# Graph-network layer on one core: convolution groups of 116 columns from whole batches, and of 116 to 136 columns from parts of one row of blocks

## The chip, the core and the metric

The kernel runs on one core of a Trainium2 chip. The core has five engines with queues of their own: TensorE (PE; PEld is its weight load) multiplies matrices into PSUM, VectorE (DVE) and ScalarE (ACT) work elementwise, GpSimd (POOL) and SyncE (SP) mostly issue DMAs here. An engine takes its instructions in the order in which they were written, and waits on semaphores for other engines and for DMAs. The metric is the device time of one execution in microseconds (us).

## The reference

x is [32, 512, 256], 32 batches of 512 nodes with 256 features; adj is a 0/1 mask [32, 512, 512]; everything is float32.

```python
h = maximum(layernorm(x), 0)
# convolution branch, per batch
c = relu(bn1(conv1d(h.T, conv1_w)))              # 1 tap, 256 -> 256 channels
c = bn2(conv1d(c, conv2_w, pad=8))               # 17 taps, 256 -> 256 channels
x_conv = relu(c + h.T).T                         # residual
# graph branch
s = h @ w_se.T + b_se                            # 3 numbers per node
A = exp(-squared_distance(s, s)) * adj
x_nmp = A @ relu(h @ w_msg.T + b_msg)
# gates (GRU cell)
gi = concat([x_conv, x_nmp]) @ w_ih.T + b_ih
gh = h @ w_hh.T + b_hh
r = sigmoid(gi_r + gh_r); z = sigmoid(gi_z + gh_z)
n = tanh(gi_n + r * gh_n)
out = x + (1 - z) * n + z * h
```

## The kernel before

**Layout.** Channels lie on the 128 partitions, in ND = 2 halves; the 512 positions of a batch lie along the free dimension. Two memory spaces matter: SBUF, and PSUM with 8 banks of 512 float32 a partition. The PSUM pools are cps (2 banks, tile ps_c), bps (1 bank, ps_b), acc (2 banks, ps_acc) and gps (3 banks, ps_g).

**The convolution of 17 taps** is done with a two-level fast scheme. A batch is cut into U = 29 blocks of Q = 18 outputs. From a group's input h1 (18 phases; one column per block, channel half and batch), VectorE forms 25 operands x2 (`fives` twice: five combinations of combinations); each operand is multiplied with its own combination of weights w, and 25 products are added into 9 sums y (`summed`, `both`). The weights of the 25 products are made once, during group 0, and kept in DRAM (WD); later groups load them again, 768 KB a product. A group is G = 4 whole batches, so 4 x 29 = 116 columns and NG = 8 groups; each row of blocks has one spare column (V = 30).

In group 0 a product is 16 matmul calls of two terms. From group 1 on it is three small products: psb (tile ps_b) of the operand's middle with the sum of both weights, which ScalarE copies out as mid, and two products of the differences xd (`ends`, VectorE), which fill the two halves of one bank ps_c. `both` adds mid to both halves and brings them to SBUF (VectorE). That makes 12 matmul calls; each float32 matmul call is two instructions on TensorE, so 24 instructions a product. Both cps banks alternate from product to product. `sums.send(done)` hands product n to `both` after ps_b of product n+1.

When a group is done, `evacuate` (ScalarE, batch norm folded in) writes each batch's 512 outputs per channel half from y into a tile xconv, of which there are four; it waits with batch b until batch b - 4 has passed its gates. `convolution` waits before the sixth product of a group until all evacuations of the last one are done.

**The other streams** are Python generators: `rows` (conv1 of a batch, which fills h1), `begins` (norm and transpose of a batch, hT, also stored in DRAM as hd), `graphs` (messages, kernel matrix, masks; its result goes to DRAM as nd) and `gates` (per batch 36 products in the order ps_r, ps_h, ps_z, ps_n for each channel half o; 144 instructions on TensorE). The gates need hTb (h again, from hd), xnb (from nd) and xconv. At the head of a batch, `residual` adds hTb to xconv on VectorE, then ScalarE applies relu; the first gate products run beside it, the products with xconv wait for it.

**Order.** A planner written out in the kernel orders the work while it is built. It keeps a model time `now` and, per engine, the time `free`; it always takes the next piece of the stream whose clock is least among those that are ready (`streams` holds each stream's rate and offset). `fill` slips VectorE background work in (norms, operands, weights, `sum_some`) as long as VectorE's model time is less than 1.5 us ahead, and `LATER` holds actions with due times. This order is what each engine's queue gets; real waits come from semaphores.

Two helpers carry nearly all instructions, so the profile names their lines: L127 for every matmul, L118 for every VectorE and ScalarE operation, L132 for transposes on TensorE. L740 are the kernel matrix's small matmuls, L929 the stores of the output, L768 the stores of nd.

Of the kernel before, what the change touches and what calls it, by code (L numbers as in the profile page):

```python
# [8 lines left out]
F32 = mybir.dt.float32  # L9
# [24 lines left out]
V = U + 1  # L34
Q = 18
TURNED = 8
# [8 lines left out]
def kernel(  # L45
# [27 lines left out]

    nc = tc.nc
# [3 lines left out]
    NG = B // G  # L78
    NR = ND * G
    NU = G * U  # L80
    NH = ND * NU
    NZ = 2 * NH
    RV = NR * V
# [5 lines left out]
    cps = ctx.enter_context(tc.tile_pool(name="cps", bufs=2, space=PSUM))  # L89
# [67 lines left out]
    XD_ = {b: dram.tile([N, D], F32, name=f"xd{b}") for b in range(TURNED, B)}  # L157
    ND_ = {(b, d): dram.tile([P, N], F32, name=f"nd{b}_{d}") for b in range(B) for d in range(ND)}
# [25 lines left out]
    def load_gates(b):  # L184
        if b >= B or b in HB:
            return
        HB[b] = late.tile([P, ND, N], F32, name="hTb", bufs=2)
        nc.sync.dma_start(HB[b], HD[b])

# [47 lines left out]
    h1 = const.tile([P, Q, NR, V], F32)  # L237
    for q, v in ((slice(0, LEAD), slice(0, 1)), (slice(Q - 1, Q), slice(V - 2, V - 1)), (slice(0, Q), slice(V - 1, V))):
        nc.gpsimd.memset(h1[:, q, :, v], 0.0)
# [88 lines left out]
    def conv1(b, o):  # L328
        hT = HT[b] if b < G else HR[b]
        ps = bank()  # L330
        matmul_sum(ps, [(w1[:, i, o * P : (o + 1) * P], hT[:, i, :]) for i in range(ND)])

        r, h = o * G + b % G, V - 2
        blocks = ps[:, : Q * h].rearrange("p (v q) -> p q v", q=Q)
        for dst, src in (
            (h1[:, LEAD:, r, :h], blocks[:, :LEAD, :]),
            (h1[:, :LEAD, r, 1 : h + 1], blocks[:, LEAD:, :]),
            (h1[:, LEAD : LEAD + N - Q * h, r, h], ps[:, Q * h :]),
        ):
            act.activation(  # L340
                dst, src, AF.Relu, bias=bn1_sh[:, o : o + 1], scale=bn1_sc[:, o : o + 1],
            )


    def fives(src, n, new):
# [8 lines left out]
        def sub(dst, a, b):  # L354
            some = n if a < 3 else n - 1
            dve.tensor_tensor(dst[:, :some, :], get(a, some), get(b, some), op=ALU.subtract)
            if a > 2:
                at = [src[:, 3 * n - 3 + b, :], flat[:, (b - 3) * RV + 1 : (b - 2) * RV + 1]]
                dve.tensor_tensor(
                    dst[:, some, :], flat[:, (a - 3) * RV + 1 : (a - 2) * RV + 1], at[b > 2],  # L360
                    op=ALU.subtract,
                )
# [7 lines left out]
        for a, b in ((2, 0), (4, 2)):  # L370
            t = new()
            sub(t, a, b)
            yield None
            if b == 0:
                less2(t, t, d1)
            else:
                less2(t, d1, t)
            yield t
# [11 lines left out]
    def operands():  # L390

        for x1 in fives(
            h1.rearrange("p q r v -> p q (r v)"), 6,
            lambda: cv.tile([P, 6, RV], F32, name="x1", bufs=3),
        ):
            yield None
            if x1 is not None:
                yield from fives(x1, 2, lambda: cv.tile([P, 2, RV], F32, name="x2", bufs=6))

    def ends(x2):  # L400

        xd = cv.tile([P, 2, RV], F32, name="xd", bufs=2)
        d0 = x2[:, 0, :]
        d02 = bass.AP(d0.tensor, d0.offset, [d0.ap[0], (1, 2), (1, RV)])
        dve.tensor_tensor(
            xd, d02, x2[:, 1:2, :].to_broadcast([P, 2, RV]), op=ALU.subtract
        )
        return xd
# [83 lines left out]
    SUMS = []  # L492

    def sum_all():
        while SUMS:
            SUMS.pop(0)()
        settle()

    def summed(g):

        y = None

# [13 lines left out]
        def both(dst, got):  # L518

            ps, mid = got  # L520
            if mid is None:
# [3 lines left out]
                dst.rearrange("p (h n) -> p h n", h=2), ps.rearrange("p (h n) -> p h n", h=2),  # L525
                mid[:, None, :].to_broadcast([P, 2, NH]), op=ALU.add,
            )

        for j1 in ORDER:
            got = yield  # L530
            n3 = cv.tile([P, NZ], F32, name="n", bufs=3)
# [3 lines left out]
            z = cv.tile([P, 3, NZ], F32, name="z")  # L535
# [7 lines left out]
            n2 = cv.tile([P, NZ], F32, name="n", bufs=3)  # L543
            both(n2, got)
            got = yield
            n1 = cv.tile([P, NZ], F32, name="n1")
# [3 lines left out]
            add(zends, zends, n1[:, None, :].to_broadcast([P, 2, NZ]))  # L550
            more(z[:, 1, :], n3, 2.0, n2)
            if j1 == 3:
                y = cv.tile([P, 3, 3, NZ], F32, name="y")
# [9 lines left out]
            (dve.free + 0.3, y, b, o) for b in range(g * G, (g + 1) * G) for o in range(ND)  # L563
# [4 lines left out]

    def evacuate():

        t, y, b, o = EVAC[0]
        if now < t or b >= G and b - G not in gated or act.free > now + 0.3:
            return False
        EVAC.pop(0)
        if o == 0:
            XC[b] = late.tile([P, ND, Q * U], F32, name="xconv", bufs=4)
        c = o * NU + b % G * U
        act.activation(
            XC[b][:, o, :].rearrange("p (u h k) -> p k h u", h=2, k=9),
            y.rearrange("p e f (h n) -> p (e f) h n", h=2)[:, :, :, c : c + U],  # L580
            AF.Identity, bias=bn2_sh[:, o : o + 1], scale=bn2_sc[:, o : o + 1],
        )
        if o == ND - 1:
            evacuated[b] = act.free + LAG
# [3 lines left out]
    XC, evacuated, gated = {}, {}, set()  # L588
# [4 lines left out]
    def all_operands():  # L593
        for _ in range(NG):
            yield from operands()
# [27 lines left out]
    def convolution():  # L623
# [3 lines left out]
        def sides(t, first=0):  # L627
            return t.rearrange("p (r v) -> p r v", v=V)[:, :, first : first + U]

        def product(ps, *terms):  # L630

            for o in range(ND):
                matmul_sum(
                    ps[:, o * NU : (o + 1) * NU].rearrange("p (b u) -> p b u", u=U),
                    [
                        (w[:, k, i, o * P : (o + 1) * P], rows[:, i * G : (i + 1) * G, :])
                        for k, rows in terms
# [3 lines left out]

        for g in range(NG):
            sums = summed(g)
            next(sums)
            done = None
            for n in range(25):
                at_product = m = 25 * g + n
                if n == 5:
                    yield lambda: not EVAC
# [7 lines left out]
                for k in (m, m + 1):  # L657
                    if 25 <= k < len(X2) and k not in XD:
                        XD[k] = ends(X2[k])
# [6 lines left out]
                ps = cps.tile([P, N], F32, name="ps_c")[:, :NZ]  # L666
                if g == 0:
                    d0, d1, d2 = sides(x2[:, 0, :]), sides(x2[:, 1, :]), sides(x2[:, 0, :], 1)
                    product(ps[:, :NH], (0, d0), (1, d1))
                    if done is not None:  # L670
                        sums.send(done)
                    yield now
                    product(ps[:, NH:], (0, d1), (1, d2))
                    mid = None
                else:
                    psb = bps.tile([P, N], F32, name="ps_b")[:, :NH]
                    product(psb, (2, sides(x2[:, 1, :])))
                    mid = cv.tile([P, NH], F32, name="mid", bufs=2)
                    act.activation(mid, psb, AF.Copy)
                    if done is not None:  # L680
                        sums.send(done)
                    yield now
                    for k in range(2):
                        product(ps[:, k * NH : (k + 1) * NH], (k, sides(XD[m][:, k, :])))
                    del XD[m]
                WS[m] = X2[m] = None
                done = ps, mid
                at_product = m + 1
                yield now
            sums.send(done)  # L690
# [135 lines left out]
    def rows(b):  # L826
        nonlocal made, made_at
        for o in range(ND):
            conv1(b, o)
            if o == ND - 1 and b % G == G - 1:  # L830
                made, made_at = b // G + 1, act.free + LAG
# [36 lines left out]
    def gates(b):  # L868
# [25 lines left out]

        def residual():
            xconv = XC.pop(b)[:, :, :N]
            dve.tensor_tensor(xconv, xconv, hT, op=ALU.add)
            yield dve.free + 0.3
            act.activation(xconv, xconv, AF.Relu)
            x_in.extend([xconv[:, i, :] for i in range(ND)] + [XN[b, d] for d in range(ND)])  # L900
# [35 lines left out]
        for o in range(ND):  # L936
# [30 lines left out]
            if o == 0:  # L967
                yield lambda: b in evacuated
                yield evacuated[b]
                yield from residual()  # L970
                yield from products(ps_r, o, 0, 0, 1, (0, 2))
                yield act.free + LAG
# [7 lines left out]
            if o == 0:  # L980
                load_gates(b + 1)
            ps_n = acc.tile([P, N], F32, name="ps_acc")
# [16 lines left out]
        gated.add(b)  # L999
# [4 lines left out]
    def sum_some():  # L1004
        if not SUMS:
            return False
        SUMS.pop(0)()
        return True

    def norm_ahead(early=0.45):  # L1010
        for b in list(NORMS)[:2]:
            if (b < G or clock["conv"] >= (b - G) / G - early) and norm_some(b):
# [40 lines left out]
    def all_rows():  # L1053
        nonlocal rows_wait
        for b in range(B):
            if b < G:
                yield from begin(b)
                yield act.free + LAG
            else:
                yield lambda: freed >= b // G - 1 and begun > b  # L1060
# [3 lines left out]
            yield from rows(b)  # L1064
            rows_wait = False

    def all_gates():
# [9 lines left out]
        "begins": (all_begins(), 4.2, -0.15),  # L1077
        "graphs": (all_graphs(), 49.0, 0.0),
        "conv": (convolution(), 66.0, 0.0),
        "gates": (all_gates(), 125.0, 1.25),  # L1080
# [19 lines left out]
    spare = cv.tile([P, 3, 3, NZ], F32, name="y").rearrange("p e f n -> p (e f n)")  # L1100
# [84 lines left out]
```

## Time and profile before

| | |
|---|---|
| median of 4 runs | 2148.93 us (2144.97 to 2149.88) |
| the profiled execution | 2147.35 us, its span 2145.5 us |
| TensorE busy | 2090.0 us (97%), 9200 instructions; weight loads 1293.8 us |
| VectorE busy | 1525.5 us (71%) |
| ScalarE busy | 761.6 us (35%) |
| GpSimd busy | 298.8 us (14%) |
| DMA | 367.12 MB, mean 171 GB/s; the queue that SP issues to carries 282.95 MB |

The page of a profile gives busy times by engine, then 40 slices of the span (each digit is tenths of busy time). The chain of waits follows the work that ended last back to its start. A group of instructions has the form: line, engine, operation, out<-in, shape, count | busy time of the group, mean ns of one | idle time of the engine before them and what ended it. Matmuls overlap in the pipeline, so the mean of one (277 ns for 116 columns) is longer than the time by which the next one follows; how long one holds the engine is read from the chain, or from the group's busy time over its count.

### The profile page before, as it was taken

Reading aid. Unit: us, or ns where it says so; the run is one execution under the profiler, and the core shown is the slowest. Engines: PE = TensorE matmul, PEld = TensorE weight load, DVE = VectorE, ACT = ScalarE, POOL = GpSimd, SP = SyncE. Lnnn points to the kernel's source line nnn. Section 1 sums busy time; section 2 is a strip of 40 time slices with the busy share of each in tenths; the row PEclk is TensorE's granted clock in tenths of the full one; section 3 lists DMA queues with packets and bytes.
Section 4 is the critical chain, followed back from the end, with each engine's and each line's share of the span. In section 5 each row is a group of like instructions: output and inputs, shape, how many; then the busy total and the mean of one; then the engine's idle time right before and its main releaser. Section 6 shows DMA issues by size and latency. Waiting matters only on the chain.

```text
span 2145.5 us, 26566 instructions
## 1 busy us (share of the span) xinstructions
PE 2090.0 (97%) x9200; PEld 1293.8 (60%) x9200; DVE 1525.5 (71%) x2820; ACT 761.6 (35%) x1277; POOL 298.8 (14%) x446
## 2 busy tenths in 40 slices
PE   8988989999999999999999999999999999999998
PEld 4876666566665666556665666656665566665443
DVE  6897778677776877667885777767776677776333
ACT  5635432433233442234324252342522334222311
POOL 2100121111111111101111111110111010011111
PEclk9999999999999999999999999999999999999999
DMA  7446666657676576766766757766675565554232
GB/s 277 178 162 240 190 188 187 206 161 195 160 211 182 157 191 192 203 167 182 199 178 187 210 134 200 198 180 177 177 195 148 152 165 153 143 156 95 59 69 40
DMA packets 539478, 367.12 MB, mean 171 GB/s; under 512 B 455248, under 2 KB 472016, under 8 KB 538704
## 3 DMA queue, kind: packets, MB, share of 16 engines
q1 hardware_dynamic: 511408, 282.95, 48.9%
q0 software_dynamic: 23248, 69.23, 10.3%
q10 hardware_dynamic: 4688, 13.24, 1.6%
q8 instruction: 73, 1.20, 0.2%
q14 instruction: 61, 0.50, 0.1%
HBM read 282.74 MB, written 82.58 MB: 170 GB/s over the span
## 4 chain that ended last, share of the span: by engine, by line
PE 83%; ACT 1%; DVE 1%; issue 0%; DVEq 0%; ACTq 0%
PE ps_acc L127 44%; PE ps_g L127 17%; PE ps_c L127 14%; PE ps_b L127 7%; PE ps_b L740 1%; PE ps_g L132 1%; ACT at L118 0%; DVE xconv L118 0%; ACT xconv L118 0%; ACT L118 0%; DVE r L118 0%; DVE o_sb L118 0%; PE ps_g L740 0%; DVE msg L118 0%; DVE res L118 0%
## 5 line engine op out<-in xcount | busy, mean ns | idle before, releaser
L127 PE MATMUL ps_acc<-xconv,wih 128*128 128x512 f32 (+1 forms) x772 | 362.6, 592 | 5.2 <-ACT xconv L118 5.2
L127 PE MATMUL ps_acc<-xnb,wih 128*128 128x512 f32 (+1 forms) x772 | 362.5, 592 | 0.0
L127 PE MATMUL ps_acc<-hTb,whh 128*128 128x512 f32 x768 | 355.5, 593 | 0.1
L127 PE MATMUL ps_c<-xd,w 128*128 128x116 f32 x2800 | 344.3, 277 | 5.2 <-DVE z L118 5.2
L127 PEld LDWEIGHTS ps_c<-xd,w 128*128 128x128 f32 x2800 | 329.9, 193 | 7.9 <-DVE z L118 5.5
L929 POOL DMA_DIRECT2D out_dram<-res x252 | 164.2, 657 | 908.7 <-DVE res L118 854.5
L118 DVE TENSOR_TENSOR r<-ps_acc,r 128x512 f32<-128x512 f32 (+1 forms) x65 | 44.4, 683 | 337.4 <-PE ps_acc L127 337.4
L127 PEld LDWEIGHTS ps_acc<-xnb,wih 128*128 128x128 f32 x772 | 142.0, 189 | 164.4 <-issue 163.5
L127 PEld LDWEIGHTS ps_acc<-xconv,wih 128*128 128x128 f32 x772 | 141.6, 190 | 158.9 <-issue 147.8
L127 PE MATMUL ps_g<-at,msg 128*128 128x512 f32 x512 | 229.2, 598 | 4.9 <-DVE at L118 4.9
L127 PEld LDWEIGHTS ps_acc<-hTb,whh 128*128 128x128 f32 x768 | 141.6, 190 | 147.7 <-issue 143.3
L127 PEld LDWEIGHTS ps_b<-x,w 128*128 128x128 f32 x1400 | 181.9, 191 | 73.2 <-issue 55.6
L118 ACT ACTIVATE mid<-ps_b 128x232 f32<-128x232 f32 x175 | 63.9, 365 | 377.3 <-PE ps_b L127 344.7
L127 PE MATMUL ps_b<-x,w 128*128 128x116 f32 x1400 | 183.6, 274 | 6.7 <-ACT at L118 6.7
L127 PEld LDWEIGHTS ps_g<-at,msg 128*128 128x128 f32 x512 | 96.9, 192 | 122.1 <-issue 113.5
L118 DVE SCALAR_TENSOR_TENSOR x<-x,x 128x480 f32<-128x480 f32 (+1 forms) x184 | 144.1, 783 | 3.4
L118 DVE TENSOR_TENSOR x<-x 128x240 f32<-128x240 f32 (+1 forms) x320 | 134.3, 461 | 0.6
L127 PE MATMUL ps_g<-wmsg,hTg 128*128 128x259 f32 x496 | 124.5, 383 | 0.0
L127 PE MATMUL ps_g<-hT,w 128*128 128x512 f32 x256 | 119.4, 610 | 1.2 <-ACT at L118 1.2
L118 ACT ACTIVATE z<-ps_acc,brz 128x512 f32<-128x512 f32 x64 | 44.0, 687 | 214.3 <-PE ps_acc L127 214.2
L127 PEld LDWEIGHTS ps_g<-wmsg,hTg 128*128 128x128 f32 x496 | 92.9, 191 | 43.0 <-issue 31.8
L118 DVE TENSOR_TENSOR xd<-x 128x480 f32<-128x480 f32 x175 | 113.1, 648 | 3.3 <-PE ps_c L127 3.3
(109 smaller groups left out, 2475.7 us busy)
## 6 DMA issues: line engine op xcount, KB each, us to landing
w<-wd SPq DMA_DIRECT2D x150, 768.0 KB, 5.6
m_sb<-in_adj_dram SPq DMA_DIRECT2D x384, 64.0 KB, 2.6
hd<-hT POOLq DMA_DIRECT2D x32, 512.0 KB, 6.1
hTb<-hd SPq DMA_DIRECT2D x32, 512.0 KB, 4.9
xnb<-nd SPq DMA_DIRECT2D x64, 256.0 KB, 2.9
res<-in_x_dram SPq DMA_DIRECT2D x256, 64.0 KB, 3.1
out_dram<-res POOLq DMA_DIRECT2D x252, 64.0 KB, 3.2
hTg<-hd SPq DMA_DIRECT2D x31, 512.0 KB, 4.3
```

What stands on the lines that cost most here:

```text
L118: getattr(self.engine, name)(*tiles, **more)
L127: nc.tensor.matmul(ps, lhsT, rhs, **more)
L132: nc.tensor.transpose(ps, a, ident)
L740: nc.tensor.matmul(pss[c], gr.left[k, :], gr.right[k, :], start=True, stop=True, tile_position=(32 * c, 0),)
L929: queue.dma_start(OB[b][:, s.start // 32 : s.stop // 32, o * P + 32 * g : o * P + 32 * g + 32], y[at, s].rearrange("i (k j) -> i k j", j=32),)
```

## The change

The batches are laid side by side as one row of 32 x 29 = 928 blocks, which is cut at 116, 251, 386, 522, 657, 792: seven groups, of 116, 135, 135, 136, 135, 135 and 136 columns. A cut may fall inside a batch; such a batch's conv1 runs twice, each time for the columns that its group needs. Between channel halves there is one spare column, and the zeros at the batches' ends are set for each group (`zeros`, on GpSimd). A product's halves have up to 272 columns each, and both do not fit one bank; ps_c becomes one tile of two banks, and there is one of it (cps has bufs=1). In group 0, where 232 + 232 columns fit a bank, products alternate between its two banks. `hand` gives a product to `both` at once (0.3 us of model time later) or, at the latest, after the next ps_b.

Evacuation goes into small tiles part (three of them), from which a DMA on POOL's queue brings the piece to DRAM (CD, `cd`). `load_conv` brings a batch's xconv back (SP's queue, two tiles), while the batch before is at its gates; `residual` adds and applies relu there, after the ps_z products of the batch before's second half. The tiles for x1 and n are fewer (2 for 3), n1 lies in z. The planner's offsets and rates follow the new group length; the gates' offset goes from 1.25 to 1.6 groups.

```diff
-V = U + 1
+STARTS = (0, 116, 251, 386, 522, 657, 792, 928)
+NG = len(STARTS) - 1
+UG = max(j - i for i, j in zip(STARTS, STARTS[1:]))
+PER = (STARTS[-1] - STARTS[1]) / (NG - 1) / U
...
-    cps = ctx.enter_context(tc.tile_pool(name="cps", bufs=2, space=PSUM))
+    cps = ctx.enter_context(tc.tile_pool(name="cps", bufs=1, space=PSUM))
...
+    CD = {b: dram.tile([P, ND, N], F32, name=f"cd{b}") for b in range(B)}
...
+    def load_conv(b):
+        if b < B and b not in XC and evacuated.get(b, 1e9) <= now:
+            XC[b] = late.tile([P, ND, N], F32, name="xconv", bufs=2)
+            nc.sync.dma_start(XC[b], CD[b])
+            XC_AT[b] = now + 7.0
+
+    def residual(b):
+        if b not in XC or b in RES or now < XC_AT[b]:
+            return
+        dve.tensor_tensor(XC[b], XC[b], HB[b], op=ALU.add)
+        RES[b] = 1e9
+
+        def relu():
+            act.activation(XC[b], XC[b], AF.Relu)
+            RES[b] = act.free + LAG
+
+        later(dve.free + 0.3, relu)
...
+    def zeros(g):
+        at = input_of(g)
+        for b in range(B + 1):
+            v = U * b - STARTS[g]
+            if 0 <= v <= sizes(g)[0]:
+                nc.gpsimd.memset(at[:, : Q if v == sizes(g)[0] else LEAD, :, v : v + 1], 0.0)
+                if v > 0:
+                    nc.gpsimd.memset(at[:, Q - 1 : Q, :, v - 1 : v], 0.0)
...
         for j1 in ORDER:
             got = yield
-            n3 = cv.tile([P, NZ], F32, name="n", bufs=3)
+            sum_all(read)
+            n3 = columns("n", bufs=2)
             both(n3, got)
...
-        t, y, b, o = EVAC[0]
-        if now < t or b >= G and b - G not in gated or act.free > now + 0.3:
+        t, y, g, b, o = EVAC[0]
+        if now < t or act.free > now + 0.3:
             return False
...
+        part = late.tile([P, Q * U], F32, name="part", bufs=3)[:, : Q * (last - first)]
         act.activation(
...
+        n0, n1 = Q * first, min(Q * last, N)
+        later(act.free + 0.4, lambda: nc.gpsimd.dma_start(CD[b][:, o, n0:n1], part[:, : n1 - n0]))
+        if o == ND - 1 and last == U:
+            evacuated[b] = act.free + 4.0
...
+        def hand():
+            nonlocal done
+            if done is not None:
+                got, done = done, None
+                sums.send(got)
...
-                if n == 5:
+                if n == 4:
                     yield lambda: not EVAC
...
-                ps = cps.tile([P, N], F32, name="ps_c")[:, :NZ]
...
+                    psb = bps.tile([P, N], F32, name="ps_b")[:, :nh]
+                    product(psb, (2, x2[:, 1, :], 0))
+                    mid = cv.tile([P, NH], F32, name="mid", bufs=2)[:, :nh]
                     act.activation(mid, psb, AF.Copy)
-                    if done is not None:
-                        sums.send(done)
+                    hand()
                     yield now
+                    ps = cps.tile([P, 2, N], F32, name="ps_c")[:, :, :nh]
                     for k in range(2):
-                        product(ps[:, k * NH : (k + 1) * NH], (k, sides(XD[m][:, k, :])))
+                        product(ps[:, k, :], (k, XD[m][:, k, :], 0))
                     del XD[m]
                 WS[m] = X2[m] = None
                 done = ps, mid
+                if g > 0:
+                    later(now + 0.3, hand)
...
             if o == 0:
-                yield lambda: b in evacuated
-                yield evacuated[b]
-                yield from residual()
+                if b not in XC:
+                    yield lambda: b in evacuated
+                    yield evacuated[b]
+                    load_conv(b)
+                yield XC_AT[b]
+                residual(b)
                 yield from products(ps_r, o, 0, 0, 1, (0, 2))
-                yield act.free + LAG
+                yield lambda: RES[b] < 1e9
+                yield RES[b]
...
             if o == 0:
                 load_gates(b + 1)
+                load_conv(b + 1)
+            else:
+                residual(b + 1)
...
+        for g in range(1, NG):
+            for b in batches(g):
+                yield lambda: freed >= g - 1 and begun > b
+                if b == batches(g)[0]:
+                    zeros(g)
                 rows_wait = True
                 load_row(b)
                 yield now + 8.0
-            yield from rows(b)
-            rows_wait = False
+                yield from rows(g, b)
+                rows_wait = False
...
-        "begins": (all_begins(), 4.2, -0.15),
-        "graphs": (all_graphs(), 49.0, 0.0),
-        "conv": (convolution(), 66.0, 0.0),
-        "gates": (all_gates(), 125.0, 1.25),
+        "begins": (all_begins(), 1.05 * PER, -0.15),
+        "graphs": (all_graphs(), 11.5 * PER, 0.0),
+        "conv": (convolution(), 80.0, 0.0),
+        "gates": (all_gates(), 31.25 * PER, 1.6),
```

## The prediction

> **What bounds the kernel now.** I read the shares by engine first, then the slices and TensorE's waits, then the chain of waits.
>
> ```profile
> PE 2090.0 (97%) x9200; PEld 1293.8 (60%) x9200; DVE 1525.5 (71%) x2820; ACT 761.6 (35%) x1277; POOL 298.8 (14%) x446
> ...
> PE   8988989999999999999999999999999999999998
> ...
> DVE  6897778677776877667885777767776677776333
> ```
>
> TensorE works 97% of the span, nearly evenly. VectorE follows at 71%, with most load early: 83.08 us of the 100 between 300 and 400 us. TensorE's own waits are few:
>
> ```profile
> PE ps_b L127 <- ACT at L118: 6.7, 8, 1.6
> PE ps_acc L127 <- ACT xconv L118: 5.2, 4, 1.4
> PE ps_c L127 <- DVE z L118: 5.2, 2, 3.0
> PE ps_g L127 <- DVE at L118: 4.9, 3, 2.7
> ```
>
> (us, times, longest.) So the kernel becomes faster only through less TensorE work, as long as no new waits appear. How long one instruction holds TensorE is read from the chain of waits in stretches without gaps (start us, us, what):
>
> ```profile
> 606.77 0.88 PE ps_b L127 x8
> 607.65 1.79 PE ps_c L127 x16
> 609.44 5.16 PE ps_acc L127 x12
> ...
> 638.00 0.88 PE ps_g L127 x4
> ```
>
> ```profile
> 664.88 0.55 PE ps_g L132 x5
> ```
>
> Per instruction: 512 columns take 5.16/12 = 430 ns, 259 columns (the messages) 0.88/4 = 220 ns, 128 columns (transposes) 0.55/5 = 110 ns, and the convolution's 116 columns 2.67/24 = 111 ns. From 128 columns up, time goes with columns at 0.839 ns (430/512), and a small rest: 259 x 0.839 = 217, 128 x 0.839 = 107. But 116 columns should take 97 ns, and take as long as 128. There is a floor, and the convolution lies on it. The groups of instructions name a likely floor:
>
> ```profile
> L127 PE MATMUL ps_c<-xd,w 128*128 128x116 f32 x2800 | 344.3, 277 | 5.2 <-DVE z L118 5.2
> L127 PEld LDWEIGHTS ps_c<-xd,w 128*128 128x128 f32 x2800 | 329.9, 193 | 7.9 <-DVE z L118 5.5
> ```
>
> The weight loads fill 329.9 us of the 344.3 us of these matmuls: each 116-column matmul needs a load of 128 weight columns, and this load is as long as it.
>
> **The change, part by part.** The sum is made against the profiled execution, 2147.35 us (span 2145.5), which lies 1.6 us below the median of the four runs.
>
> *Fewer, wider products.* Group 0 stays at 116 columns. Behind it 7 groups of 25 products become 6, at 135 or 136 columns (mean 135.3). Before: 175 products x 24 instructions x 111.3 ns = 467 us. After: 150 x 24 = 3600 instructions. By the slope one takes 135.3 x 0.839 = 113.5 ns, with the rest of 2.5 ns that 128 and 259 columns show 116 ns; 3600 x 116 = 418 us. Gain 49 us. The ends: 113.5 ns gives 58 us; if the 14 ns above the streaming time were a cost of every instruction and no floor, 135.3 columns would take 127.5 ns and the gain would be 8 us. I take 116, since 128 columns are nearest and show no such cost.
>
> *VectorE work* of the convolution has the same columns in fewer instructions. Its operations x take 653 ns for 480 columns and 1651 for 1440, so 154 ns of each are fixed; the changed kernel issues 2660 VectorE instructions where 2820 were: 160 x 154 ns = 25 us less. VectorE is not on the path, so this only makes room.
>
> *One buffer for a product's output instead of two.* A product's two halves now have a bank each, and there is one pair: product n+1 may not write ps_c before VectorE has added mid and read product n out. One such read of 464 columns took 632 ns; 540 take some 715. Behind the waiting matmul stand all others, on an engine that keeps its order. What covers it is the TensorE work between the two. From the new order of TensorE, with the durations above: in 137 of the 150 products 2.6 us or more stand between, mostly 6 to 8. In 10 only the next product's ps_b (8 x 116 ns = 0.93 us) stands between, in 3 more 1 to 2.6 us; all 13 lie in group 1 and the first two thirds of group 2, where VectorE is fullest. The same kernel before has 6 such close pairs, and the two waits for z (2.20 and 2.96 us) are among them although it has two buffers. So a close pair costs at least 5.2/6 = 0.87 us, and at most about 3.0. I take 1.5, as only part of VectorE's queue is ahead of the read: 13 x 1.5 = 19.5, less the 5.2 of before: +14 us (ends +6 and +34). Why not more elsewhere: VectorE's longest wait in sum is the one for ps_acc, 402.4 us, so it is mostly ahead of TensorE.
>
> [...] The order of the instructions says that other streams' matmuls cover the evacuation in 137 cases.
>
> *Residual made ahead.* Its add and relu stood between a batch's last products and the next's. The chain shows what that cost once TensorE had nothing else:
>
> ```profile
> 2039.40 0.69 DVE r L118
> 2040.09 1.14 DVE xconv L118
> ...
> 2041.26 1.07 ACT xconv L118
> ...
> 2042.37 29.46 PE ps_acc L127 x68
> ```
>
> The four waits sum to 5.2 us. They now run a stage earlier, beside the ps_n products (8 x 430 ns = 3.4 us, more than 1.14 + 1.07). Gain 5 us (0 to 6); next in line there is nothing late.
>
> *Outputs through DRAM.* 72 pieces instead of 64 evacuations (1323 ns each on ScalarE, before and after); each then goes out on POOL's queue, and 32 loads of 512 KB come in on SP's. Three piece buffers: ScalarE's fourth must wait until the first has left. Nearest row: 256 KB stores of nd from POOL land 2.9 and 2.5 us after issue; issue itself takes some 0.57 us. So a buffer is busy 1.3 + 3.5 + about 0.5 us, while two more evacuations take 2.6: ScalarE can be held 0 to 2 us each time, and with it mid and the gate sigmoids queued behind. ScalarE is 35% busy and TensorE has two ps_acc banks (1.7 us of products to a bank), so only the excess shows. Ends 0 and 72 x 0.5 = 36; I take +4, as the nearest rows (mid starting promptly behind 1.3 us evacuations without a TensorE wait for it) lie near zero. On SP the new load waits for the store, with the loads of w and masks behind it; it is issued only when the planner thinks the piece is out, and 25 loads of 768 KB disappear: 0 (to +5). POOL gains 72 issues of 0.6 us and 64 tiny memsets at 14% load: 0 to 3, I take 1; behind them in its queue stand out_dram and nd, which nobody waits for soon.
>
> [...]
>
> *Seams.* Four batches are split by a group's end: their conv1 is computed with 18 columns of overlap, 32 instructions x 15 ns: +0.5 us, and 4 more loads of hT. Group 1 needs five batches instead of four before it can start, group 2 six; a load and rows take about 10 us a batch, in place of 40 us now 50 to 60, against about 8 products (some 90 us) between the freeing of h1 and its next need. The start of group 1 (TensorE worked 91.06 of 100 us between 200 and 300) can lose up to 10: I take +3.
>
> Sum: -49 + 14 - 5 + 4 + 1 + 0.5 + 3 = -31.5, so 2147.35 becomes 2116; against the median of the runs that is 2117.
>
> **Rivals.**
> 1. *Nothing new shows*: the close pairs fall together with waits that exist anyway. -58 - 6: 2083 to 2095. For it: VectorE gets lighter. Against: 13 close pairs where it is fullest.
> 2. *ScalarE is held by the pieces*, or the trip through DRAM is late for the gates: another +20: 2132 to 2144. For: pieces follow each other in the new order of ScalarE, with mid between them. Against: other streams stand ready.
> 3. *Slower: the single output buffer.* If reads come late not in 13 but in most products, the convolution pays each time. It decides from (49 + 5 - 8)/150 = 0.31 us a product; at 0.5 us: 2147 - 46 + 75 = 2176. For: the read is queued behind whatever VectorE has, up to two or three operations of 0.7 to 1.7 us. Against: 6 to 8 us between.
> 4. *The floor is none* (8 us gain): 2147 - 8 - 5 + 22 = 2156. Against: the 110 ns of 128 columns.
>
> **Chances and range.** Forecast (2097 to 2132) 0.57, as its terms are rows and counts; rival 1 0.14; rival 2 0.14; rival 3 0.09; rival 4 0.04; 0.02 other. 0.2% (4.3 us) is about what the runs tell from no change. Same gets 0.03, from the upper part of rival 2 and from rival 4; slower 0.11; faster 0.86. Range 2088 to 2150: rivals 3, 4 and a part of 1 stay outside. Likeliest alone: 2097 to 2132.
>
> **What would show it.** ps_b and ps_c of 135 columns at 2.75 to 2.8 us a product; 3600 instructions where 4200 were; waits of ps_c for n and z of 10 to 30 us, between 200 and 560 us; no waits for xconv in the last batches; ScalarE waiting for DMAs before its pieces, with TensorE hardly touched. Waits for ps_c spread over the whole span, or a pitch over 120 ns, would prove me wrong.

## The result and the profile after

The changed kernel takes 2151.54 us (median of 47 runs, 2145.14 to 2163.55), the kernel before 2148.7 (71 runs); the ratio is 1.0015, 95% interval 1.0009 to 1.0021. The forecast of 2117 us is wrong: nothing was gained. The ratio of an experiment below is taken to the kernel before as measured beside it (2150.2 to 2150.4 us). The span of the profiled execution is 2149.8 us.

The page after, the lines that answer to those of before:

```profile
PE 2058.6 (96%) x8632; PEld 1258.2 (59%) x8632; DVE 1513.0 (70%) x2660; ACT 762.2 (35%) x1271; POOL 337.3 (16%) x582
...
PE   8888799999998999999999999999999999999998
...
DVE  6787578777876677885777876877667777754333
```

TensorE is busy 31 us less, and the span is 4 us longer. The chain of waits between 1200 and 1260 us shows that a product became what was forecast:

```profile
1219.13 0.92 PE ps_b L135 x8
1220.05 1.84 PE ps_c L135 x16
1221.89 1.72 PE ps_acc L135 x4
```

0.92 + 1.84 = 2.76 us for 24 instructions, 115 ns each; 150 products take 414 us, where 175 of 2.67 us took 467. So 53 us of work are gone. Yet TensorE is busy only 31 us less, and it is idle 36 us more (span less busy time: 91.2 us, before 55.5). So the gain was lost in two ways: in waits, and in work that runs more slowly. The mean clock that TensorE was granted in the two profiled executions is 0.987 of full speed, and 0.994 before; 0.7% of 2059 us would be 14 us, an estimate. Over all 47 runs of the changed kernel it is 0.982 to 0.989 (median 0.986), in the 39 runs of the kernel before beside the experiments 0.989 to 0.994 (median 0.990). TensorE's waits after (us in total, times, longest):

```profile
PE ps_c L135 <- ACT z L126: 11.2, 13, 2.5
PE ps_c L135 <- DVE n L126: 8.9, 3, 4.4
PE ps_c L135 <- ACT n L126: 7.7, 10, 2.5
...
PE ps_b L830 <- ACT right L126: 6.1, 2, 4.8
PE ps_c L135 <- issue: 5.1, 2, 2.7
PE ps_acc L135 <- DMA xnb<-nd: 5.1, 1, 5.1
...
PE ps_g L135 <- DMA hT<-hd: 3.4, 1, 3.4
PE ps_c L135 <- DVE z L126: 3.4, 1, 3.4
PE ps_acc L135 <- ACT xconv L126: 2.7, 1, 2.7
PE ps_b L135 <- DMA w<-wd: 2.7, 1, 2.7
```

Where they lie is seen in the busy time by stretch (stretch, its length, then TensorE busy; the other columns are the weight loads, VectorE, ScalarE, GpSimd, TensorE's clock, DMA share, GB/s). Before:

```profile
50.00:250.00 200.00, 181.51 (x1166) 143.53 (x1165) 161.88 (x319) 103.31 (x183) 20.12 (x26) 0.97 0.53 187
250.00:800.00 550.00, 542.40 (x2437) 340.64 (x2436) 412.11 (x769) 192.71 (x324) 87.47 (x129) 0.99 0.66 186
800.00:2000.00 1200.00, 1194.93 (x5147) 728.61 (x5147) 871.32 (x1574) 408.70 (x673) 159.02 (x233) 1.00 0.63 171
```

After:

```profile
50.00:250.00 200.00, 167.45 (x1047) 133.33 (x1045) 141.13 (x282) 95.02 (x175) 20.21 (x35) 0.95 0.49 173
250.00:800.00 550.00, 514.00 (x2269) 326.41 (x2270) 416.51 (x736) 184.61 (x322) 93.19 (x157) 0.98 0.68 196
800.00:2000.00 1200.00, 1195.36 (x4826) 711.02 (x4825) 868.53 (x1472) 427.25 (x678) 189.09 (x322) 1.00 0.65 179
```

From 800 to 2000 us nothing is lost. Between 50 and 800 us TensorE idles 18.5 + 7.6 us in the kernel before and 32.5 + 36.0 after: 42 us more, at a slightly lower clock too. Two places were named from the trace and tried.

**Group 0.** One stretch in order of time, after (start, us, engine, line, operation; in brackets the idle time before it and what ended it; the last row is cut by the end of the stretch), TensorE and then ScalarE:

```profile
155.80 1.94 PE L135 MATMUL ps_c<-x,w 128*128 128x116 f32 x16
158.39 2.04 PE L135 MATMUL ps_c<-x,w 128*128 128x116 f32 x16 [0.65 <-ACT n L126]
160.27 0.60 PE L140 MATMUL ps_g<-ident,m_sb 128*128 128x128 f32 x4
160.70 1.94 PE L135 MATMUL ps_c<-x,w 128*128 128x116 f32 x16
163.29 0.93 PE L135 MATMUL ps_c<-x,w 128*128 128x116 f32 x6 [0.65 <-ACT z L126]
```

```profile
157.78 0.56 ACT L126 ACTIVATE n<-ps_c 128x464 f32<-128x464 f32 x1 [6.31 <-PE ps_c L135]
...
162.68 0.56 ACT L126 ACTIVATE z<-ps_c 128x464 f32<-128x464 f32 x1 [1.75 <-PE ps_c L135]
```

A product of group 0 has 32 instructions, 16 to a half. ScalarE reads the product before, from the other bank, but starts only when the first half of this one has ended, and the second half starts only when that read has ended. The two banks are one tile now (`two`), the read is written between the halves, and it looks as if each is ordered against the whole tile; the first experiment tests that. Group 0's matmuls as a group, before and after (the idle time ahead of them stands behind the second bar):

```profile
L127 PE MATMUL ps_c<-x,w 128*128 128x116 f32 x800 | 95.0, 278 | 6.9 <-DVE x L118 2.7 <-ACT w L118 2.2 <-DVE sq L118 1.9
```

```profile
L135 PE MATMUL ps_c<-x,w 128*128 128x116 f32 x800 | 103.8, 286 | 22.5 <-ACT z L126 11.2 <-ACT n L126 7.7 <-ACT w L126 2.2
```

**Groups 1 and 2.** The idle time ahead of ps_c, and its longest wait, VectorE and then TensorE (the last row is cut by the end of the stretch):

```profile
L135 PE MATMUL ps_c<-xd,w 128*128 128x135 f32 x1600 | 206.8, 283 | 19.4 <-DVE n L126 8.9 <-issue 5.1 <-DVE z L126 3.4
```

```profile
591.52 1.35 DVE L126 TENSOR_TENSOR xd<-x 128x544 f32<-128x544 f32 x2
592.79 0.71 DVE L126 TENSOR_TENSOR z<-z,n 128x540 f32<-128x540 f32 x1
...
595.56 1.28 DVE L126 TENSOR_TENSOR z<-z 128x1080 f32<-128x1080 f32 x1
596.88 0.72 DVE L126 SCALAR_TENSOR_TENSOR z<-n 128x540 f32<-128x540 f32 x1
597.70 0.72 DVE L126 TENSOR_TENSOR n<-ps_c,mid 128x540 f32<-128x540 f32 x1
```

```profile
593.08 1.08 PE L135 MATMUL ps_b<-x,w 128*128 128x135 f32 x8
598.57 1.81 PE L135 MATMUL ps_c<-xd,w 128*128 128x135 f32 x10 [4.41 <-DVE n L126]
```

VectorE works nearly without a break (busy for 7.76 of the 8 us from 590 to 598), but the read of ps_c stands behind the sums of the products before: `sum_all(read)`, new with the change, puts them ahead of the first read of each five, since there are fewer n tiles. That is read from the order alone; no run left it out.

### The profile page after: what moved, and what is told of

The parts are those of the page before. It is cut to its first block, busy times and chain, and to the rows that moved or that the text cites. A ratio compares the mean times of both kernels' runs of the same rounds, so it can differ in the third digit from the quotient of the medians.

```text
span 2149.8 us, 25648 instructions
## 1 busy us (share of the span) xinstructions
PE 2058.6 (96%) x8632; PEld 1258.2 (59%) x8632; DVE 1513.0 (70%) x2660; ACT 762.2 (35%) x1271; POOL 337.3 (16%) x582
## 4 chain that ended last, share of the span: by engine, by line
PE 67%; ACT 1%; DVE 1%; DMA 0%; SPq 0%; issue 0%; DVEq 0%
PE ps_acc L135 39%; PE ps_g L135 13%; PE ps_c L135 9%; PE ps_b L135 5%; PE ps_b L830 1%; PE ps_g L140 1%; DMA hT<-hd 0%; ACT at L126 0%; SPq L868 0%; ACT L126 0%; ACT h L126 0%; DVE o_sb L126 0%; DMA xnb<-nd 0%; ACT r L126 0%; SPq L310 0%
## 5 line engine op out<-in xcount | busy, mean ns | idle before, releaser
L135 PE MATMUL ps_c<-xd,w 128*128 128x135 f32 (+1 forms) x2400 | 307.9, 282 | 19.4 <-DVE n L126 8.9
L135 PEld LDWEIGHTS ps_c<-xd,w 128*128 128x128 f32 x2400 | 293.5, 193 | 22.3 <-issue 14.3
L135 PEld LDWEIGHTS ps_b<-x,w 128*128 128x128 f32 x1200 | 159.7, 190 | 66.9 <-issue 54.3
L135 PE MATMUL ps_b<-x,w 128*128 128x135 f32 (+1 forms) x1200 | 164.4, 279 | 7.4 <-ACT at L126 3.6
L126 ACT ACTIVATE mid<-ps_b 128x270 f32<-128x270 f32 (+1 forms) x150 | 59.6, 398 | 263.0 <-PE ps_b L135 262.9
L126 DVE SCALAR_TENSOR_TENSOR x<-x,x 128x544 f32<-128x544 f32 (+5 forms) x161 | 137.6, 855 | 2.9
L126 DVE TENSOR_TENSOR msg<-ps_g,bmsg 128x256 f32<-128x256 f32 x128 | 53.8, 421 | 112.0 <-PE ps_g L135 111.3
L126 DVE TENSOR_TENSOR x<-x 128x272 f32<-128x272 f32 (+5 forms) x280 | 127.7, 497 | 0.3
L135 PE MATMUL ps_g<-hT,w 128*128 128x512 f32 (+4 forms) x288 | 123.4, 573 | 4.6 <-DMA hT<-hd 3.4
L135 PE MATMUL ps_c<-x,w 128*128 128x116 f32 x800 | 103.8, 286 | 22.5 <-ACT z L126 11.2
```

Source lines behind the costliest of these rows:

```text
L126: getattr(self.engine, name)(*tiles, **more)
L135: nc.tensor.matmul(ps, lhsT, rhs, **more)
```

## The experiments

**Group 0 with two tiles.** A pool of two single banks serves group 0 and is closed behind it.

```diff
...
-                two = cps.tile([P, 2, N], F32, name="ps_c")
...
-                    ps, mid = two[:, n % 2, :nz], None
+                    ps, mid = cps.tile([P, N], F32, name="ps_c")[:, :nz], None
```

> The changed kernel, but group 0 takes its products' outputs in two tiles of one bank, as the kernel before did; the pool is closed after group 0 and the one tile of two banks follows. Theory A: in group 0 the second half of a product waits for ScalarE's read of the product before, because both banks are one tile and the read is ordered against the whole tile, although it reads the other bank. Those waits (22.5 us of idle time before ps_c of 116 columns, where the kernel before has 6.9) vanish: 2151.5 - 20 to 25 = 2127 to 2132, and group 1 starts some 20 us earlier than 270. Theory B: in group 0 VectorE's operands are the limit (82 of 100 us busy between 100 and 200 us), so the wait moves to x: 2146 to 2152.

Measured: 2136.68 us, 0.9937 (0.9922 to 0.9952) of the kernel before, 15 us under the changed kernel. The idle time ahead of these matmuls (last number) nearly goes:

```profile
L136 PE MATMUL ps_c<-x,w 128*128 128x116 f32 x800 | 99.7, 285 | 3.6 <-ACT w L127 2.2 <-DVE x L127 1.2 <-ACT n L127 0.2
```

The order of instructions on TensorE is the changed kernel's, so the ordering against the whole tile alone cost this. It is less than theory A's 20 to 25 us: group 0 ends 18 us earlier (by its last product, 204 in place of 222 us), but ahead of group 1 some of it is lost again.

**The planner leaves room for the read.** Each product of group 1 and later waits in the planner until VectorE's read of the last is nearly due.

```diff
...
                 got, done = done, None
                 sums.send(got)
+                read_at = dve.free
...
                 yield now
+                if g > 0 and n < 24:
+                    yield lambda: done is None
+                    yield read_at - 0.8
```

> The changed kernel, but from group 1 on the planner does not take up the next product before VectorE's read of the last one is due to end within the time of the next ps_b. No two products then stand with less than 2 us of other TensorE work between them, where the changed kernel has 13 such pairs. Theory A: the waits of ps_c of 135 columns (19.4 us idle) and the clock dips behind them go: 2127 to 2134. Theory B: between 250 and 800 us TensorE simply has too little to do (operands, gates and loads arrive late), and the idle time comes back elsewhere: 2146 to 2152.

Measured: 2128.40 us, 0.9895 (0.9881 to 0.991), 23 us under the changed kernel, as theory A said. The idle time ahead of ps_c of 135 columns falls from 19.4 us to 1.4:

```profile
L135 PE MATMUL ps_c<-xd,w 128*128 128x135 f32 x1600 | 202.0, 279 | 1.4 <-DVE n L126 1.4
```

Not all of the 23 us is this wait. In the new order the waits for DMAs of xnb, hT and w, 11.2 us in the changed kernel, fall to 1.7 as well, those for right and at (products of the graph branch) rise from 9.7 to 18.3. In all TensorE idles 20 us less (71.0) and is busy 4 us less.

**A control: room between products where there are two buffers.** The kernel before, `yield now + 2.5` after each product from group 1 on.

> The kernel before, where the planner leaves 2.5 us of its time after each product from group 1 on. A control for spaced. Theory A (the single output buffer makes close pairs dear): with two buffers there is little to win, the 5.2 us of waits for z: 2143 to 2150. Theory E (spacing the products helps whatever the buffers, since it spreads VectorE's load): 2125 to 2135.

Measured: 2157.35 us, 1.0033 (1.0024 to 1.0042): slower than before. So a fixed pause after each product does not help, and theory E falls; theory A's 2143 to 2150 is missed too, by 7 us. The 5.2 us of waits of ps_c for z that it was to save are gone from the list of waits, but four waits that the kernel before does not have took their place: 2.7 us of ps_b for w, 2.4 of ps_g for nothing that the profile shows, 2.3 of ps_acc for r and 2.2, in two, of ps_g for aug. The pause here is fixed, where the remedy waits for the read; it is a control for spacing, not the same edit.

**Group 0's fault put into the kernel before.** Its group 0 takes alternating banks of one tile.

```diff
...
+                ps = two[:, n % 2, :NZ] if g == 0 else cps.tile([P, N], F32, name="ps_c")[:, :NZ]
```

> The kernel before, with one edit: group 0's products go alternately into the two banks of one tile. Theory A (order against the whole tile): 2148.7 + 18 to 24 = 2167 to 2173, with waits of ps_c for ScalarE's n and z of about 0.65 us each in group 0. Theory B (VectorE's operands limit group 0): 2148 to 2155.

Measured: 2162.25 us, 1.0048 (1.0031 to 1.0065), 12 us more. The waits are those of the changed kernel, 14.1 us of idle time ahead of these matmuls in place of 6.9:

```profile
L128 PE MATMUL ps_c<-x,w 128*128 128x116 f32 x800 | 104.4, 289 | 14.1 <-ACT n L119 7.2 <-ACT z L119 4.6 <-ACT w L119 2.2
```

The mechanism of theory A stands in both directions, 15 us taken out and 12 put in; its size of 18 to 24 was too large. The 11.8 us of new waits for n and z replace 4.6 us of old ones for VectorE's x and sq, so that 7.2 us remain. In the profiled execution, the slowest of the four, the same instructions also keep TensorE busy longer (2103.3 us, before 2090.0).

**All of the change but the wide groups.** Eight groups of 116 columns, two buffers of one bank.

```diff
-STARTS = (0, 116, 251, 386, 522, 657, 792, 928)
+STARTS = tuple(range(0, 929, 116))
-    cps = ctx.enter_context(tc.tile_pool(name="cps", bufs=1, space=PSUM))
+    cps = ctx.enter_context(tc.tile_pool(name="cps", bufs=2, space=PSUM))
...
```

> The changed kernel with eight groups of 116 columns, whose product fits one bank, and two such tiles; outputs through DRAM, residual ahead, evacuation pieces and planner stay. Theory A (the loss is the output banks in group 0 and behind it): the rest of the change is worth its residual, -5 us, and costs up to 8 for the trip through DRAM: 2142 to 2152, with TensorE idle before 800 us as in the kernel before (27 us above its work). Theory C (the trip through DRAM and the planner's new offsets starve TensorE early): 2160 to 2175.

Measured: 2147.58 us, 0.9985 (0.9974 to 0.9996). The trip through DRAM, the residual ahead and the new offsets together are worth 3 us at this width; theory C falls.

**The same with one buffer.** As the last, but from group 1 on one bank; TensorE's order stays.

```diff
...
+            if g == 1:
+                first_ctx.close()
+                cps = ctx.enter_context(tc.tile_pool(name="cps", bufs=1, space=PSUM))
...
```

> narrow (eight groups of 116 columns, the rest of the change kept), but from group 1 on one output bank in place of two; group 0 keeps two. The order on TensorE is the same, instruction for instruction, so the price of the single buffer stands alone. There are 7 close pairs (6 with only ps_b between, one with 1 to 2 us). Theory A (only close pairs pay, 1.5 to 3 us each with the clock dip behind them): 2147.6 + 8 to 20 = 2155 to 2168, waits of ps_c for VectorE's n and z of 8 to 20 us, before 800 us. Theory F (every product pays a little): 175 x 0.3 us or more, 2200 and above, with waits all over the span.

Measured: 2166.83 us, 1.0076 (1.0061 to 1.0091), 19 us over its twin. The idle time ahead of ps_c, first with two buffers, then with one:

```profile
L135 PE MATMUL ps_c<-xd,w 128*128 128x116 f32 x2800 | 342.9, 276 | 0.0
```

```profile
L136 PE MATMUL ps_c<-xd,w 128*128 128x116 f32 x2800 | 348.2, 278 | 16.1 <-DVE z L127 5.5 <-issue 5.1 <-DVE n L127 4.6
```

This is the price of the single buffer by itself: 19 us. The waits ahead of ps_c, 16 us more, are not simply added to the time; all but two of them lie before 480 us. The pages, first with two buffers, then with one:

```profile
PE 2095.8 (98%) x9200; PEld 1297.3 (60%) x9200; DVE 1527.0 (71%) x2820; ACT 760.3 (35%) x1275; POOL 331.2 (15%) x579
```

```profile
PE 2106.0 (97%) x9200; PEld 1307.9 (60%) x9200; DVE 1528.7 (71%) x2820; ACT 761.0 (35%) x1275; POOL 331.2 (15%) x579
```

The spans are 2146.3 and 2166.1 us. Some other waits shrank, so TensorE idles only 9.6 us more (60.1, before 50.5), and the same 9200 instructions keep it busy 10.2 us longer, at a mean granted clock of 0.987, with two buffers 0.990. Half of the price is slower work. Theory F (every product pays) is wrong.

**Both remedies.**

> The two edits of g0_two_tiles and spaced together. Theory A (two separate places of loss, 15 us in group 0 and 23 us behind it): 2151.5 - 38 = 2113, 2108 to 2120. Theory B (one shortage early in the kernel that only shows in different places): about the better of the two alone, 2124 to 2130.

Measured: 2110.06 us, 0.9814 (0.9793 to 0.9834). The two add up: 15 + 23 = 38 was expected, 41 came. This version beats both kernels, at 40 us under the kernel before.

**Evacuation paced, alone and on top.** `evacuate` also waits until 4.5 us of model time after ScalarE ended with the third-last piece.

```diff
...
-        if now < t or act.free > now + 0.3:
+        if now < t or act.free > now + 0.3 or len(SENT) > 2 and now < SENT[-3] + 4.5:
...
+        SENT.append(act.free)
...
```

> The changed kernel with that pacing alone. Theory A: 2151.5 - 4 to 10. Theory D: 2148 to 2153.

> both, and the planner starts the evacuation into a piece buffer only 4.5 us of model time after ScalarE ended with that buffer's last piece, so that ScalarE need not stand still for the store (part waited 20.9 us for DMAs in the changed kernel, and TensorE 4.6 to 4.8 us for right behind it, where group 1 begins). Theory A: those waits for right go, 4 to 10 us less than both. Theory D (ScalarE's waits are hidden but for that one): within 3 us of both; slower if later pieces make the gates wait.

Measured: alone 2150.74 us, 1.0004 (0.9994 to 1.0014); with both remedies 2115.82, 0.9837 (0.9817 to 0.9857), 6 us slower than without it (2111.00 to 2117.61 in four runs, 2107.57 to 2112.28 without). ScalarE's wait for the pieces' stores falls only from 20.9 to 15.3 us, and from 17.4 to 16.3. The wait for right ahead of group 1 shrank from 4.8 to 0.8 us on top of both, without a gain in time. Theory A's saving is not there.

**The residual at its old place**, in the version with both remedies.

```diff
...
                 load_conv(b + 1)
-            else:
-                residual(b + 1)
```

> both, without the call that makes the next batch's residual ahead: add and relu run at the head of each batch's gates, as in the kernel before. If the residual's step was sized rightly (four or five last batches, 1.3 us each, nothing elsewhere): 2110 + 5 to 7 = 2115 to 2117, with waits of ps_acc for xconv in the last batches. If it also mattered while other streams run: 2125 or more. If nothing was won by it: 2108 to 2112.

Measured: 2134.28 us, 0.9933 (0.9914 to 0.9951), 24 us more than with it. I had expected 5 to 7; the other branch, that it also matters while other streams run, is what came. TensorE waits for xconv not only in the last batches:

```profile
PE ps_acc L136 <- ACT xconv L127: 20.5, 13, 2.9
```

In the kernel before these were 4 waits and 5.2 us. Five of the 13 waits, 1.3 us each, are those of the last batches; the other eight come earlier. With the wide groups the residual ahead is worth far more than its cost there showed; why the planner's order hides it less here was not settled.

## Why the prediction was wrong

The sum of the forecast, term by term:

| term | forecast | shown |
|---|---|---|
| fewer, wider products | -49 | -53 (2.67 to 2.76 us a product, 25 fewer) |
| residual ahead | -5 | -5: the four waits for xconv in the last batches are gone (one of 2.7 us at 262 us is new) |
| group 0 | not in the sum | +15 (two tiles), +12 put into the kernel before |
| one output buffer | +14 | +23 (spaced, other waits included) at the new width, +19 at 116 columns |
| pieces, seams, the rest | +8.5 | about +18, by difference |

*Fewer, wider products* was right, and with it the floor: 135 columns cost 115 ns, 116 had been said. Rival 4 is out.

*Group 0 stays at 116 columns* is the step that failed first: group 0 was put at nothing, and cost 15 us. It was read from the width, and the output tiles of group 0 were passed over: the diff makes two tiles into one tile of two banks. The banks still alternate, so it looked equal; but what reads and writes waited for went by the tile: with one tile 22.5 us of idle time stand ahead of these matmuls, with two 3.6. The first half of product n+1, the read of n and the second half form a chain, which the instruction order of the changed kernel shows. A forecast has to go through each tile that is merged and ask what is now ordered.

*One buffer instead of two* had the right mechanism, and as waiting time the right size: the idle time ahead of ps_c is 19.4 us, as 13 close pairs at 1.5 us had given, 14.2 more than the 5.2 of before. That both factors fit is luck: the time lies in nine waits of 0.6 to 4.4 us. What was mis-sized is the price: a pause was counted at its length and nothing else. The run with a single bank lost 19 us, half of it as slower work; spacing won 23, of which 18 are this wait. The place was right: all these waits lie before 800 us, and rival 3, a loss in most products, did not happen.

*Outputs through DRAM* and *seams* were too small, 8.5 against about 18. The last is not measured by itself: it is what remains of the 58 us of work and residual after the version with both remedies gained 40 of them (2110.06 against 2150.36 us). The profile of that version says what kind of loss it is:

```profile
PE 2050.8 (97%) x8632; PEld 1254.6 (60%) x8632; DVE 1510.6 (72%) x2660; ACT 761.6 (36%) x1271; POOL 336.7 (16%) x582
```

Of its span of 2107.6 us TensorE is idle 56.8, about as in the kernel before (55.5), although the waits for right, behind the pieces, have grown from 0.7 to 11.3 us. But it is busy only 39 us less than before, where 53 us of work are gone. So some 14 us of the rest are slower work and not waiting. The mean granted clock is 0.987, before 0.994, which by estimate is 0.7% of 2051 us, 14 us; by the medians of the runs (0.987 and 0.990) it is 6 us. The clock is lowest in group 0 and where group 1 starts: 0.92 between 50 and 250 us, in the kernel before 0.97. What lowers it there was not tested.

In the changed kernel xnb, hT and w are waited for too, none of which cost TensorE anything of note before; the longest of these, 5.06 us for xnb, stands behind loads of x in SP's queue, after which the load was issued only at 664.2 us. With both remedies xnb is down to 1.9 us, and hT and w are gone from the list. The run with narrow groups loses only 2 or 3 us to the trip through DRAM, so that it needs the wide groups, with their five or six batches to a seam, to hurt; pacing the evacuations did not cure it. Which part is the longer seam and which the queues is open.

The sum with the shown terms is -53 - 5 + 15 + 23 + 18 = -2, where +2.8 was measured. Its last term is taken from the version with both remedies, so the sum checks only that these two add up (41 us came, not 38), not what the rest is made of. VectorE's work fell by 12.5 us, not by the 25 that were worked out; nothing rested on it.

None of the rivals named what happened: I had put 0.03 on no change, and two losses in different places met the gain.

The 72 stores of pieces, issued by GpSimd, landed 3.2 us after issue in the median (2.1 to 7.5). The 64 stores of nd, issued by GpSimd too, took 4.2 and 3.1 us in the median, before 2.9 and 2.5.

## What to carry to other kernels

When a change merges buffers, list for every merged tile which reads and writes are now ordered against each other, also in the stages that the change seems to leave alone. A single output buffer was paid for here where the filling engine came back before the reader (19 us at 116 columns), so count those places in the new instruction order and make the planner keep them apart: here the two together turned a change worth nothing into one worth 1.9%. Compare busy time as well as waits, for the same instructions: here half the price of a single buffer was slower work.

## What was not expected of the hardware

Behind some pauses of TensorE its granted clock was lower. In the changed kernel it stood 5.06 us before 667.67; the chain then has

```profile
667.67 3.65 PE ps_acc L135 x4
```

Four matmuls of 512 columns took 3.65 us, and take 1.72 elsewhere. By stretch (TensorE's clock is the third number from the end):

```profile
662.00:668.00 6.00, 0.94 (x3) 0.33 (x2) 5.82 (x11) 0.00 (x0) 2.51 (x4) 0.97 0.94 191
668.00:673.00 5.00, 5.00 (x20) 3.02 (x20) 1.13 (x2) 1.08 (x2) 0.07 (x1) 0.69 0.91 236
```

The granted clock was 0.69 in these 5 us, and the four matmuls took nearly 2 us more. Between 598 and 603 us, behind the pause of 4.41 us ahead of ps_c shown above, it was 0.66. The length of one pause does not decide it, though. The next rows follow a pause of 3.17 us and one of 1.62 us:

```profile
655.40:660.40 5.00, 5.00 (x24) 3.33 (x25) 1.18 (x2) 0.45 (x1) 0.00 (x0) 1.00 0.62 123
1117.60:1122.60 5.00, 5.00 (x26) 4.76 (x27) 0.00 (x0) 1.78 (x4) 0.00 (x0) 0.66 0.77 148
```

Behind the longer one the clock stayed at 1.00, behind the shorter one it was 0.66; what decides it was not shown. A pause of 0.65 us in group 0, in the stretch shown above, is followed by 16 matmuls in 2.04 us, where 16 with no pause ahead of them took 1.94.
